# Placing matmuls and evictions one by one in an attention and experts kernel: turns in pairs, content next to the q terms, another layout for the position terms

## Chip, cores and metric

The kernel runs on one core of a Trainium2 chip. The metric is device time in microseconds (us) of the whole launch, the median of three runs. A profiled execution of the same kernel gives the trace; its own time is given beside its span, which runs from the first to the last instruction.

## What is computed

An adaptive layer norm, attention with relative position terms, a second norm and a mixture of experts, all in float32, with 16 sequences of 512 tokens, width 256, 16 heads of 16, and 8 experts of which each token uses two:

```python
h = layernorm(x) * (1 + ca) + sa
q, k, v = heads(h @ Wq + bq), heads(h @ Wk + bk), heads(h @ Wv + bv)
rel_q = einsum('bhld,lrd->bhlr', q, pos_emb)          # pos_emb[l, r] = dist_emb[l - r + 255]
rel_k = einsum('bhrd,lrd->bhlr', k, pos_emb)
scores = (q @ k.T + rel_q + rel_k) / sqrt(16)
x = x + ga * norm(softmax(scores) @ v @ Wo + bo + h)  # with gamma, beta
h = layernorm(x) * (1 + cb) + sb
x = x + gb * sum_over_the_two_best_experts(h @ w_e.T + b_e)
```

A negative index counts from the table's end, one beyond the end takes the last row.

## The kernel before

**Two stretches.** A first stretch norms the input, makes q, k and v and puts them into DRAM, turns q and k into stationary operands for the position terms (`stationary`), and computes the first ten blocks of these terms (`blocks`, LEAD = 10). Then comes the main loop, which works through 64 units. A unit is 128 query rows of one sequence. It goes through four groups g of four heads; t counts the heads of a group.

**Position terms.** `q_set` (L156) makes rel_q of 16 query rows in four banks of PSUM: 8 matmuls, two for each of four 32-row parts of TensorE (L165, bank names pq). ScalarE copies them to the tile r (L175). `k_set` (L177) makes rel_k with 16 matmuls into four banks pk (L186), and VectorE adds them to r (L195). `store` (L199) writes r to the DRAM tensor rel_d, one DMA of 1 MB for each quarter g. In the main loop each of the first 54 units also makes one block of these terms, ten units ahead of its use; the last ten make none.

**A group of heads.** `load_scores` (L577) reads the position terms of four heads into the tile s, one DMA of 1 MB. `content` (L637) makes q k^T of the four heads in four banks qk, each on 32 rows of TensorE (L644); VectorE adds s to each bank, scales, and takes the maximum (L650), then turns the maximum's sign (L654). `exps` (L657) is ScalarE's exponential in place. `turn` (L664) turns a head's 128 x 512 probabilities on TensorE, four 128 x 128 transposes into one bank pt (L669), and ScalarE copies them out as pT (L671). `context` (L674) multiplies by v, 16 matmuls of 32 columns into the bank pc (L684); a column of ones in v gives the sums of the softmax.

**A unit's rest.** `back` and `contextT` (pcl, pct) bring the context into the layout for the projection; `project` (ph, L727 and L732) adds h and multiplies by Wo, copies the sum out as x2 and starts the first norm; `residual`, `norm2` and `modulate` (fpt) give the experts' input, `route` (fpl) and `mask_t` (fpmt) the two chosen experts, `bias` (fpb) the biases, and `experts` the products with two experts at a time in the bank fpy (L827), four times a unit. `expert_sums` weighs one half on VectorE (L838) and one on ScalarE (L842). `sqrt_inv` (L99) raises to the power -1/2 on GpSimd (POOL), after an addition on VectorE (L100).

**Banks.** All but pc take their banks from one pool of seven; the eighth is pc's. Of the free banks a new tile gets the one that was released longest ago, in the order of the program.

**What sets the order.** The order is written by hand: every step has a slot and a rank in it, and the program is the list sorted by both. Each engine runs its own instructions in that order, and so does SP's queue, which issues nearly all DMAs. A unit starts a new round every 16 slots, so groups are four slots apart and steps of two or three units stand among one another (z is the unit's first slot, q0 a group's):

```python
            at(q0 - 12, 0, load_scores, u, g)
            at(q0 - 4, 5, content, u, g)
            at(q0 - 2, 7, exps, u, g, (0, 1))
            at(q0 - 1, 7, exps, u, g, (2, 3))
            for t in range(4):
                at(q0 + t, 3, turn, u, g, t)
            at(q0 + 5, 4, context, u, g)
```

with `q_set` at z + 2 + 4g (rank 4), `k_set` at z + 15 + 4g (rank 2), `experts` at z + 18 + 4 pr (rank 6) and `store` at z + 28 + 2g. In one slot, evictions stand directly behind the matmuls that they empty, since one function holds both.

Of the kernel before, what the change touches and what calls it, by code (L numbers as in the profile page):

```python
# [11 lines left out]
ALU = mybir.AluOpType  # L12
# [22 lines left out]
def adaln_attention_moe_kernel(  # L35
# [79 lines left out]
    rel_d = [dram.tile([P, P, S], F32, tag=f"rel_{n}", name=f"rel_d{n}") for n in range(8)]  # L115
# [10 lines left out]
    class Rel:  # L126
# [29 lines left out]
        def q_set(self, n, g):  # L156

            s, lb, rb, lh = self.at(n)
            e = self.qe[(lb * 2 + lh, g // 2)]
            bs = [bank(f"pq_{n}_{g}_{t}") for t in range(4)]  # L160
            for a in range(2):
                for t in range(4):
                    lp = lb * P + lh * LQ + 16 * g + 8 * a + 2 * t
                    m0 = S - 1 - lp + rb * RK
                    nc.tensor.matmul(  # L165
                        bs[t][:, a * 256 : (a + 1) * 256],
                        e[32 * t : 32 * t + 32, (g % 2) * 2 + a, :],
                        t_r[32 * t : 32 * t + 32, :, m0 : m0 + RK],
                        start=True, stop=True,
                    )  # L170
            dst = self.two[n % 2][:, 16 * g : 16 * g + 16, :].rearrange(
                "p (a t i) r -> p t a (i r)", a=2, t=4
            )
            for t in range(4):
                nc.scalar.copy(dst[:, t], bs[t].rearrange("p (a c) -> p a c", a=2))  # L175

        def k_set(self, n, g):  # L177
# [14 lines left out]
            for t in range(4):  # L192
                o = 32 * g + 8 * t
                dst = self.two[n % 2][:, :, o : o + 8]
                nc.vector.tensor_tensor(  # L195
                    dst, bs[t].rearrange("p (r l) -> p l r", r=8), dst, ALU.add
                )

        def store(self, n, g):  # L199

            s, lb, rb, lh = self.at(n)
            l0 = lh * LQ + 16 * g
            nc.sync.dma_start(
                out=rel_d[s * 4 + lb][:, l0 : l0 + 16, rb * RK : (rb + 1) * RK],
                in_=self.two[n % 2][:, 16 * g : 16 * g + 16, :],
            )
# [4 lines left out]
    with ExitStack() as pro:  # L211
# [163 lines left out]
        def blocks(n):  # L375
# [6 lines left out]
            for g in range(4):  # L382
                rel.q_set(n, g)
                for w in ahead:
# [3 lines left out]
            for g in range(4):  # L388
                rel.k_set(n, g)
                for w in ahead:  # L390
# [186 lines left out]
    def load_scores(u, g):  # L577
# [4 lines left out]
        nc.sync.dma_start(  # L582
            out=st, in_=rel_d[s * 4 + lb][h0 : h0 + 7 : 2].rearrange("h l r -> l h r")
        )
# [52 lines left out]
    def content(u, g):  # L637
# [4 lines left out]
        for t in range(4):  # L642
# [3 lines left out]
            )  # L646
        mx = u3.tile([P, 4], F32, tag="mx", name=f"mx_{u}_{g}")
# [16 lines left out]
    def turn(u, g, t):  # L664
        t_ = units[u]
        pt = bank(f"pt_{u}_{g}_{t}")
        for rb in range(NL):
            cols = slice(rb * P, (rb + 1) * P)
            nc.tensor.transpose(pt[:, cols], t_["s", g][:, t, cols], ident)  # L669
        pT = tp.tile([P, S], F32, tag="pT", name=f"pT_{u}_{g}_{t}")  # L670
        nc.scalar.copy(pT, pt)  # L671
# [49 lines left out]
    def project(u):  # L721
# [19 lines left out]
        nc.vector.bn_stats(stats, ph)  # L741
# [14 lines left out]
    def norm2(u):  # L756
# [6 lines left out]
        sqrt_inv(rstd, mv[:, 1:2], EPS_ADA)  # L763
        xn = u1.tile([P, E], F32, tag="xn", name=f"xn_{u}")
# [68 lines left out]
    def expert_sums(u, pr):  # L833
# [4 lines left out]
        nc.vector.scalar_tensor_tensor(  # L838
            t_["y"], py[:, 0:E], t_["mask"][:, e : e + 1], t_["y"], ALU.mult, ALU.add
        )  # L840
        ye = u2.tile([P, E], F32, tag=f"ye{pr > 0}", name=f"ye_{u}_{pr}")
        nc.scalar.activation(  # L842
            ye, py[:, E : 2 * E], AF.Identity, scale=t_["mask"][:, e + 1 : e + 2]
        )
# [13 lines left out]


    slots = {}  # L860

    def at(slot, order, fn, *args):
        slots.setdefault(slot, []).append((order, len(slots.get(slot, ())), fn, args))

    for u in range(NP):
        z = 16 * u
        for g in range(4):
            q0 = z + 4 * g
            at(q0 - 12, 0, load_scores, u, g)
            at(q0 - 4, 5, content, u, g)  # L870
            at(q0 - 2, 7, exps, u, g, (0, 1))
            at(q0 - 1, 7, exps, u, g, (2, 3))
            for t in range(4):
                at(q0 + t, 3, turn, u, g, t)
            at(q0 + 5, 4, context, u, g)
        at(z - 16, 0, lambda u: units.setdefault(u, {}), u)
        at(z - 13, 0, load_k, u, 0)
        at(z - 6, 0, load_k, u, 1)
        at(z - 15, 0, load_q, u)
        at(z - 7, 0, mask_q, u)  # L880
        at(z - 9, 0, load_rest, u)
        at(z + 15, 0, load_tail, u)
        z += 16
        at(z + 3, 6, back, u)
        at(z + 5, 3.5, contextT, u)
        at(z + 7, 6, project, u)
        at(z + 8, 0, residual, u)
        at(z + 10, 0, norm2, u)
        at(z + 11, 6, modulate, u)
        at(z + 13, 7, route, u)  # L890
        at(z + 15, 7, mask_t, u)
        at(z + 16, 7, bias, u)
        for pr in range(4):
            at(z + 18 + 4 * pr, 6, experts, u, pr)
            at(z + 19 + 4 * pr, 1, expert_sums, u, pr)
        at(z + 35, 0, finish, u)
# [3 lines left out]
        if n < NP:  # L900
            for g in range(4):
                at(z + 2 + 4 * g, 4, rel.q_set, n, g)
                at(z + 15 + 4 * g, 2, rel.k_set, n, g)
            for g in range(4):
                at(z + 28 + 2 * g, 0, rel.store, n, g)
        if n + 1 < NP:
            for w in rel.wants(n + 1):
                o = 8 + w[3] if w[0] == "q" else (16, 17, 21, 25)[w[2] % 2 * 2 + w[3]]
                at(z + o, 0, rel.load, w)
    for n in range(min(slots), max(slots) + 1):  # L910
        for _, _, fn, args in sorted(slots.get(n, ()), key=lambda e: e[:2]):
            fn(*args)
# [49 lines left out]
```

## Time and profile before

| | |
|---|---|
| Median of 3 runs | 2932.14 us (2932.07 to 2933.13) |
| Profiled execution: its time | 2935.72 us |
| Its span | 2934.0 us, mean granted TensorE clock 0.971 |
| Busy: TensorE (PE) | 2770.9 us, 94% |
| Busy: weight loads (PEld) | 1803.2 us, 61% |
| Busy: ScalarE (ACT) | 2068.8 us, 71% |
| Busy: VectorE (DVE) | 1837.4 us, 63% |
| Busy: GpSimd (POOL) | 630.1 us, 21% |
| DMA, SP's queue | 854,032 packets, 790.03 MB, 85.2% of 16 engines |
| rel_d<-r (stores) | 256 DMAs of 1,024 KB, 8.5 us to landing |
| s<-rel_d (loads) | 256 DMAs of 1,024 KB, 7.8 us to landing |

Groups that the change moves, from the page's table of costs: pT<-pt L671 1,024 times at 584 ns, r<-pk L195 1,024 at 683 ns, s<-s L660 1,024 at 731 ns, s<-qk L650 1,024 at 685 ns, r<-pq L175 1,024 at 603 ns.

How to read it: a row of a table of costs gives line, engine, operation, tiles (out<-in), shapes and count, then busy us and the mean of one. A row of the timeline gives start and length in us, engine, line and operation; several of a kind in a row are merged, and what stands in brackets is idle time of the engine before it and what ended it. The chain of waits is followed back from the last instruction; its pieces are cut where the next begins, so their lengths are times from start to start. Matmuls are pipelined, and TensorE's busy share contains short waits inside a group of matmuls.

### The profile page before, as it was taken

Reading aid. Unit: us, or ns where it says so; the run is one execution under the profiler, and the core shown is the slowest. Engines: PE = TensorE matmul, PEld = TensorE weight load, DVE = VectorE, ACT = ScalarE, POOL = GpSimd, SP = SyncE. Lnnn points to the kernel's source line nnn. Section 1 sums busy time; section 2 is a strip of 40 time slices with the busy share of each in tenths; the row PEclk is TensorE's granted clock in tenths of the full one; section 3 lists DMA queues with packets and bytes.
Section 4 is the critical chain, followed back from the end, with each engine's and each line's share of the span. In section 5 each row is a group of like instructions: output and inputs, shape, how many; then the busy total and the mean of one; then the engine's idle time right before and its main releaser. Section 6 shows DMA issues by size and latency. Waiting matters only on the chain.

```text
span 2934.0 us, 76492 instructions
## 1 busy us (share of the span) xinstructions
PE 2770.9 (94%) x30186; PEld 1803.2 (61%) x30186; DVE 1837.4 (63%) x5140; ACT 2068.8 (71%) x3938; POOL 630.1 (21%) x863
## 2 busy tenths in 40 slices
PE   8779963999999999999999999999999999999997
PEld 5556642666666666666666666666666666665654
DVE  5446542666666666666666666666666666675553
ACT  2345432877777777777777777777777777777774
POOL 1000000022222222222222222222222222223333
PEclk9989876999999999999999999999999999999998
DMA  6879998688988998899888998889899898897561
GB/s 181 306 253 317 296 299 273 223 276 283 286 282 277 294 307 279 274 285 292 281 278 286 291 289 281 278 285 288 278 286 307 279 286 281 278 278 264 201 238 43
DMA packets 855350, 796.49 MB, mean 271 GB/s; under 512 B 25545, under 2 KB 649409, under 8 KB 854737
## 3 DMA queue, kind: packets, MB, share of 16 engines
q1 hardware_dynamic: 854032, 790.03, 85.2%
q8 instruction: 240, 3.93, 0.5%
q10 hardware_dynamic: 960, 1.57, 0.2%
q14 instruction: 118, 0.96, 0.1%
HBM read 462.20 MB, written 328.25 MB: 269 GB/s over the span
## 4 chain that ended last, share of the span: by engine, by line
PE 77%; DMA 2%; POOL 2%; DVE 1%; SPq 1%; ACT 1%; issue 1%; POOLq 0%; DVEq 0%; ACTq 0%
PE pt L669 18%; PE fpy L827 15%; PE qk L644 12%; PE pq L165 10%; PE pc L684 8%; PE pk L186 8%; PE ph L732 2%; DMA vu<-v_d 1%; PE fpl L788 1%; PE pcl L699 1%; PE fpb L818 1%; PE fpt L775 1%; POOL qm L614 1%; PE pct L716 0%; POOL rstd L101 0%
## 5 line engine op out<-in xcount | busy, mean ns | idle before, releaser
L671 ACT COPY pT<-pt 128x512 f32<-128x512 f32 x1024 | 595.3, 584 | 317.9 <-PE pt L669 295.3
L195 DVE TENSOR_TENSOR r<-pk,r 128x512 f32<-128x512 f32 x1024 | 635.0, 683 | 189.2 <-PE pk L186 164.3
L660 ACT ACTIVATE s<-s,mx 128x512 f32<-128x512 f32 x1024 | 689.7, 731 | 43.3 <-DVE mx L654 39.7
L650 DVE CUSTOM_DVE_ANT_0 s<-qk,s 128x512 f32<-128x512 f32 x1024 | 644.1, 685 | 85.8 <-PE qk L644 81.4
L669 PE MATMUL pt<-ident,s 128*128 128x128 f32 x4096 | 660.0, 284 | 10.8 <-ACT s L660 10.4
L175 ACT COPY r<-pq 128x512 f32<-128x512 f32 x1024 | 525.6, 603 | 153.9 <-PE pq L165 137.1
L669 PEld LDWEIGHTS pt<-ident,s 128*128 128x128 f32 x4096 | 450.0, 143 | 284.7 <-ACT s L660 73.8
L827 PE MATMUL fpy<-we_sb,fhT 128*128 128x512 f32 x1024 | 506.1, 617 | 0.0
L848 POOL TENSOR_TENSOR ye<-ye,ye 128x256 f32<-128x256 f32 x192 | 140.5, 732 | 1597.4 <-ACT ye L842 1105.8
L838 DVE SCALAR_TENSOR_TENSOR fy<-fpy,fmask,fy 128x256 f32<-128x256 f32 x256 | 123.5, 482 | 471.6 <-PE fpy L827 319.3
L644 PE MATMUL qk<-k,qm 32*128 32x512 f32 x2048 | 380.1, 650 | 28.0 <-POOL qm L614 28.0
L186 PEld LDWEIGHTS pk<-t_f,ke 32*128 32x128 f32 x8192 | 268.3, 190 | 189.5 <-ACT r L175 124.1
L165 PE MATMUL pq<-t_r,qe 32*128 32x256 f32 x4096 | 370.5, 409 | 4.2 <-DMA qe<-eq_d 2.8
L186 PE MATMUL pk<-t_f,ke 32*128 32x128 f32 x8192 | 319.8, 287 | 8.8 <-DVE r L195 3.6
L827 PEld LDWEIGHTS fpy<-we_sb,fhT 128*128 128x128 f32 x1024 | 175.0, 190 | 195.2 <-issue 159.8
L165 PEld LDWEIGHTS pq<-t_r,qe 32*128 32x128 f32 x4096 | 240.2, 186 | 82.4 <-issue 41.7
L684 PE MATMUL pc<-pT,vu 128*32 128x128 f32 x8192 | 279.1, 277 | 0.0
L684 PEld LDWEIGHTS pc<-pT,vu 128*32 128x32 f32 x8192 | 209.9, 110 | 44.1 <-issue 43.5
L644 PEld LDWEIGHTS qk<-k,qm 32*128 32x128 f32 x2048 | 133.4, 184 | 101.5 <-DVE r L195 47.6
L101 POOL TENSOR_TENSOR rstd<-rstd,mhalf 128x1 f32<-128x1 f32 (+1 forms) x144 | 87.9, 610 | 436.0 <-DVE rstd L100 428.1
L842 ACT ACTIVATE ye<-fpy,fmask 128x256 f32<-128x256 f32 x256 | 125.3, 490 | 51.3 <-DVE fy L838 51.3
L614 POOL TENSOR_SCALAR qm<-qs,par 128x256 f32<-128x256 f32 x128 | 117.7, 932 | 150.1 <-DMA k<-k_d 137.8
(110 smaller groups left out, 2061.7 us busy)
## 6 DMA issues: line engine op xcount, KB each, us to landing
rel_d<-r SPq DMA_DIRECT2D x256, 1024.0 KB, 8.5
s<-rel_d SPq DMA_DIRECT2D x256, 1024.0 KB, 7.8
vu<-v_d SPq DMA_DIRECT2D x64, 576.0 KB, 7.5
ke<-ek_d SPq DMA_DIRECT2D x128, 256.0 KB, 7.2
k<-k_d SPq DMA_DIRECT2D x128, 256.0 KB, 6.6
gt<-gates_d SPq DMA_DIRECT2D x64, 256.0 KB, 4.7
v_d<-v SPq DMA_DIRECT2D x16, 576.0 KB, 6.4
xt<-in_x SPq DMA_DIRECT2D x16, 512.0 KB, 5.9
```

The source lines that it names most:

```text
L165: nc.tensor.matmul(bs[t][:, a * 256 : (a + 1) * 256], e[32 * t : 32 * t + 32, (g % 2) * 2 + a, :], t_r[32 * t : 32 * t + 32, :, m0 : m0 + RK],
L175: nc.scalar.copy(dst[:, t], bs[t].rearrange("p (a c) -> p a c", a=2))
L186: nc.tensor.matmul(bs[t][:, a * 128 : (a + 1) * 128], e[32 * t : 32 * t + 32, a, :], t_f[32 * t : 32 * t + 32, :, m0 : m0 + LQ], start=Tru ...
L195: nc.vector.tensor_tensor(dst, bs[t].rearrange("p (r l) -> p l r", r=8), dst, ALU.add)
L614: nc.gpsimd.tensor_scalar(qm[:, pa], qs, par[:, pa : pa + 1], None, ALU.mult)
L644: nc.tensor.matmul(bs[t], t_["q"][rows, pa, cc, :], t_["k", cc][rows, :], start=True, stop=True)
L650: nc.vector.tensor_tensor_reduce(st[:, t, :], bs[t], st[:, t, :], 0.25, -3.0e38, ALU.add, ALU.max, mx[:, t : t + 1],)
L660: nc.scalar.activation(t_["s", g][:, t, :], t_["s", g][:, t, :], AF.Exp, bias=t_["m", g][:, t : t + 1])
L669: nc.tensor.transpose(pt[:, cols], t_["s", g][:, t, cols], ident)
L671: nc.scalar.copy(pT, pt)
L684: nc.tensor.matmul(pc[32 * t : 32 * t + 32, g, :], t_["v"][:, rb, h * VW : h * VW + 32], pTs[t][:, rb * P : (rb + 1) * P], start=(rb == 0) ...
L827: nc.tensor.matmul(py, t_["hT"][:, kc, :], we_sb[:, kc, pr * 2 * E : (pr + 1) * 2 * E], start=(kc == 0), stop=(kc == NE - 1),)
```

## The change

Every step gets a position of its own on one number line, in slots as before, from a table O. The matmuls and the evictions of `q_set`, `k_set`, `content` and `turn` become steps of their own (`q_copy`, `k_add`, `add_content`, `turn_copy`), `exps` is placed head by head, and the second norm is cut in two (`norm2` ends at the power, `normed` applies it). In TensorE's order of a group, turns of heads 2 and 1 stand together, content stands directly ahead of the q terms, and turn 3 goes between experts and the k terms. The table also moves later steps of a unit, for example `modulate` from 11 to 13.3 and `finish`, which stores the output, from 35 to 42.1. In `expert_sums` ScalarE's half is put ahead of VectorE's in the program; as both read one bank, the second waits for the first. `project` takes the norm's statistics from x2 instead of the bank.

The DRAM tensor rel_d gets another layout, with blocks of 128 columns r outside the rows l. A quarter's store then writes 8 KB in one piece from each partition, where it wrote 16 pieces of 512 bytes. A load of four heads becomes four DMAs, each reading four pieces of 512 bytes for each partition, where one DMA read 2 KB pieces.

The first stretch uses the same functions in the same order as before, with the new layout.

```diff
-    rel_d = [dram.tile([P, P, S], F32, tag=f"rel_{n}", name=f"rel_d{n}") for n in range(8)]
+    rel_d = [dram.tile([P, NL, P, RK], F32, tag=f"rel_{n}", name=f"rel_d{n}") for n in range(8)]
...
                     )
+            self.qb = bs
+        def q_copy(self, n, g, ts):
             dst = self.two[n % 2][:, 16 * g : 16 * g + 16, :].rearrange(
...
             )
-            for t in range(4):
-                nc.scalar.copy(dst[:, t], bs[t].rearrange("p (a c) -> p a c", a=2))
+            for t in ts:
+                nc.scalar.copy(dst[:, t], self.qb[t].rearrange("p (a c) -> p a c", a=2))
...
                     )
-            for t in range(4):
+            self.kb = bs
+        def k_add(self, n, g, ts):
+            for t in ts:
                 o = 32 * g + 8 * t
...
                 nc.vector.tensor_tensor(
-                    dst, bs[t].rearrange("p (r l) -> p l r", r=8), dst, ALU.add
+                    dst, self.kb[t].rearrange("p (r l) -> p l r", r=8), dst, ALU.add
                 )
...
             nc.sync.dma_start(
-                out=rel_d[s * 4 + lb][:, l0 : l0 + 16, rb * RK : (rb + 1) * RK],
+                out=rel_d[s * 4 + lb][:, rb, l0 : l0 + 16, :],
                 in_=self.two[n % 2][:, 16 * g : 16 * g + 16, :],
...
                 rel.q_set(n, g)
+                rel.q_copy(n, g, range(4))
                 for w in ahead:
...
                 rel.k_set(n, g)
+                rel.k_add(n, g, range(4))
                 for w in ahead:
...
         st = sp.tile([P, 4, S], F32, tag="s", name=f"s_{u}_{g}")
-        nc.sync.dma_start(
-            out=st, in_=rel_d[s * 4 + lb][h0 : h0 + 7 : 2].rearrange("h l r -> l h r")
-        )
+        for t in range(4):
+            nc.sync.dma_start(
+                out=st[:, t, :].rearrange("p (rb r) -> p rb r", r=RK),
+                in_=rel_d[s * 4 + lb][h0 + 2 * t].rearrange("rb l r -> l rb r"),
+            )
         units[u]["s", g] = st
...
             )
+        t_["qk"] = bs
+    def add_content(u, g):
+        t_ = units[u]
+        bs = t_.pop("qk")
         mx = u3.tile([P, 4], F32, tag="mx", name=f"mx_{u}_{g}")
...
             nc.tensor.transpose(pt[:, cols], t_["s", g][:, t, cols], ident)
+        t_["pt", g, t] = pt
+    def turn_copy(u, g, t):
+        t_ = units[u]
         pT = tp.tile([P, S], F32, tag="pT", name=f"pT_{u}_{g}_{t}")
-        nc.scalar.copy(pT, pt)
+        nc.scalar.copy(pT, t_.pop(("pt", g, t)))
         t_["p", g, t] = pT
...
         mv = u2.tile([P, 2], F32, tag="mv", name=f"mv2_{u}")
-        nc.vector.bn_stats(stats, ph)
+        nc.vector.bn_stats(stats, x2)
         nc.vector.bn_aggr(mv, stats)
...
         sqrt_inv(rstd, mv[:, 1:2], EPS_ADA)
+        t_["ln2"] = (mv, rstd)
+    def normed(u):
+        t_ = units[u]
+        mv, rstd = t_.pop("ln2")
         xn = u1.tile([P, E], F32, tag="xn", name=f"xn_{u}")
...
         e = 2 * pr
-        nc.vector.scalar_tensor_tensor(
-            t_["y"], py[:, 0:E], t_["mask"][:, e : e + 1], t_["y"], ALU.mult, ALU.add
-        )
         ye = u2.tile([P, E], F32, tag=f"ye{pr > 0}", name=f"ye_{u}_{pr}")
...
             ye, py[:, E : 2 * E], AF.Identity, scale=t_["mask"][:, e + 1 : e + 2]
+        )
+        nc.vector.scalar_tensor_tensor(
+            t_["y"], py[:, 0:E], t_["mask"][:, e : e + 1], t_["y"], ALU.mult, ALU.add
         )
...
-    slots = {}
-    def at(slot, order, fn, *args):
-        slots.setdefault(slot, []).append((order, len(slots.get(slot, ())), fn, args))
+    O = {
+        "content": -2.4626,
+        "add_content": -2.3612,
+        ("exp", 0): -1.2159,
+        ("turn", 0): -0.8732,
+        ("exp", 2): -0.5643,
+        ("exp", 1): -0.4930,
+        ("turn_copy", 0): -0.4876,
+        ("turn", 2): 0.5281,
+        ("turn_copy", 2): 0.8703,
+        ("turn", 1): 1.4758,
+        ("turn_copy", 1): 1.4814,
+        ("exp", 3): 1.6823,
+        "q_set": 2.2208,
+        ("q_copy", 2): 2.4310,
+        ("q_copy", 3): 2.5904,
+        ("q_copy", 0): 2.7341,
+        ("q_copy", 1): 2.7393,
+        "back": 2.8935,
+        ("turn", 3): 2.9973,
+        ("turn_copy", 3): 3.3249,
+        "contextT": 3.9805,
+        "context": 4.1821,
+        "project": 5.8037,
+        "residual": 6.9000,
+        "norm2": 10.4317,
+        "normed": 10.8506,
+        "modulate": 13.3163,
+        "route": 14.5204,
+        "k_set": 15.0296,
+        ("k_add", 0): 15.0864,
+        ("k_add", 1): 15.5883,
+        ("k_add", 3): 15.5900,
+        ("k_add", 2): 15.6240,
+        "mask_t": 15.8852,
+        "bias": 18.0871,
+        "experts": 18.5363,
+        "expert_sums": 18.9734,
+        "store": 27.8101,
+        "finish": 42.0757,
+    }
+    pieces = []
+    def at(pos, fn, *args):
+        pieces.append((pos, len(pieces), fn, args))
...
         z = 16 * u
+        at(z - 16, lambda u: units.setdefault(u, {}), u)
+        at(z - 13, load_k, u, 0)
+        at(z - 6, load_k, u, 1)
+        at(z - 15, load_q, u)
+        at(z - 7, mask_q, u)
+        at(z - 9, load_rest, u)
+        at(z + 15, load_tail, u)
         for g in range(4):
             q0 = z + 4 * g
-            at(q0 - 12, 0, load_scores, u, g)
-            at(q0 - 4, 5, content, u, g)
-            at(q0 - 2, 7, exps, u, g, (0, 1))
-            at(q0 - 1, 7, exps, u, g, (2, 3))
+            at(q0 - 12, load_scores, u, g)
+            at(q0 + O["content"], content, u, g)
+            at(q0 + O["add_content"], add_content, u, g)
             for t in range(4):
-                at(q0 + t, 3, turn, u, g, t)
-            at(q0 + 5, 4, context, u, g)
-        at(z - 16, 0, lambda u: units.setdefault(u, {}), u)
-        at(z - 13, 0, load_k, u, 0)
-        at(z - 6, 0, load_k, u, 1)
-        at(z - 15, 0, load_q, u)
-        at(z - 7, 0, mask_q, u)
-        at(z - 9, 0, load_rest, u)
-        at(z + 15, 0, load_tail, u)
+                at(q0 + O["exp", t], exps, u, g, (t,))
+                at(q0 + O["turn", t], turn, u, g, t)
+                at(q0 + O["turn_copy", t], turn_copy, u, g, t)
+            at(q0 + O["context"], context, u, g)
         z += 16
-        at(z + 3, 6, back, u)
-        at(z + 5, 3.5, contextT, u)
-        at(z + 7, 6, project, u)
-        at(z + 8, 0, residual, u)
-        at(z + 10, 0, norm2, u)
-        at(z + 11, 6, modulate, u)
-        at(z + 13, 7, route, u)
-        at(z + 15, 7, mask_t, u)
-        at(z + 16, 7, bias, u)
+        for fn in (back, contextT, project, residual, norm2, normed, modulate, route, mask_t, bias):
+            at(z + O[fn.__name__], fn, u)
         for pr in range(4):
-            at(z + 18 + 4 * pr, 6, experts, u, pr)
-            at(z + 19 + 4 * pr, 1, expert_sums, u, pr)
-        at(z + 35, 0, finish, u)
+            at(z + O["experts"] + 4 * pr, experts, u, pr)
+            at(z + O["expert_sums"] + 4 * pr, expert_sums, u, pr)
+        at(z + O["finish"], finish, u)
...
             for g in range(4):
-                at(z + 2 + 4 * g, 4, rel.q_set, n, g)
-                at(z + 15 + 4 * g, 2, rel.k_set, n, g)
-            for g in range(4):
-                at(z + 28 + 2 * g, 0, rel.store, n, g)
+                q0 = z + 4 * g
+                at(q0 + O["q_set"], rel.q_set, n, g)
+                at(q0 + O["k_set"], rel.k_set, n, g)
+                for t in range(4):
+                    at(q0 + O["q_copy", t], rel.q_copy, n, g, (t,))
+                    at(q0 + O["k_add", t], rel.k_add, n, g, (t,))
+                at(z + O["store"] + 2 * g, rel.store, n, g)
         if n + 1 < NP:
...
                 o = 8 + w[3] if w[0] == "q" else (16, 17, 21, 25)[w[2] % 2 * 2 + w[3]]
-                at(z + o, 0, rel.load, w)
-    for n in range(min(slots), max(slots) + 1):
-        for _, _, fn, args in sorted(slots.get(n, ()), key=lambda e: e[:2]):
-            fn(*args)
+                at(z + o, rel.load, w)
+    for _, _, fn, args in sorted(pieces, key=lambda e: e[:2]):
+        fn(*args)
 # ---- launch: one core; the host lays the inputs out and no more ----
```

## The prediction, made before the run

> **What bounds the kernel now.** I read the chain of work that ended last, then TensorE in order of time, then the cost groups, then VectorE in order of time, then the windows.
>
> ```profile
> PE 77%; DMA 2%; POOL 2%; DVE 1%; SPq 1%; ACT 1%; issue 1%; POOLq 0%; DVEq 0%; ACTq 0%
> 1519.13 1.91 PE fpy L827 x4
> 1521.04 1.10 PE pk L186 x32
> 1522.15 0.59 PE pt L669 x4
> ...
> 1523.85 0.44 PE pt L669 x4
> 1524.28 1.07 PE qk L644 x8
> 1525.35 0.59 PE pt L669 x4
> 1525.94 1.01 PE pc L684 x32
> 1526.95 0.59 PE pt L669 x4
> 1527.54 1.95 PE pq L165 x15
> 1529.49 1.91 PE fpy L827 x4
> ```
>
> These are the chain and one group of four heads in it (left out: the unit's ph). TensorE is the chain, back to back; but pq took 1.95 here, and 1.08 at best. Over units in the steady stretch (700 to 2500 us, 39.13 us a unit, 52 alike) fpy, pk and pc never vary by over 0.01 us and pt by 0.06; pq averages 1.36 against 1.08, qk 1.51 (before a pt) against 1.07. Per unit that is 1.14 + 1.32 + 0.13 = 2.6 us of waiting, and 36.5 us of work.
>
> ```profile
> 1522.16 2.49 DVE L195 TENSOR_TENSOR r<-pk,r 128x512 f32<-128x512 f32 x4 [0.60 <-PE pk L186]
> 1526.39 0.68 DVE L650 CUSTOM_DVE_ANT_0 s<-qk,s 128x512 f32<-128x512 f32 x1
> 1527.00 0.69 DVE L650 CUSTOM_DVE_ANT_0 s<-qk,s 128x512 f32<-128x512 f32 x1
> 1527.61 0.69 DVE L650 CUSTOM_DVE_ANT_0 s<-qk,s 128x512 f32<-128x512 f32 x1
> ```
>
> What it waits for is banks: seven of them, and VectorE empties one per 0.61 us. In the instructions of that stretch the held-up pq began at 1528.36, 0.75 us after the add that started at 1527.61. So an eviction frees its bank 0.75 us after it starts, and TensorE is at fpy 1.06 us after the last of pq's four banks came.
>
> ```profile
> 340.00:480.00 140.00, 80.19 (x831) 63.99 (x824) 59.51 (x138) 41.49 (x80) 0.14 (x1) 0.70 0.95 283
> 700.00:2500.00 1800.00, 1799.95 (x21055) 1168.08 (x21048) 1215.04 (x3360) 1416.74 (x2717) 436.37 (x598) 1.00 0.91 285
> 465.68 9.65 SPq L203 DMA_DIRECT2D rel_d<-r  x4
> ```
>
> Two windows (length, PE, PEld, DVE, ACT, POOL busy, clock, DMA share) and one row of SP's queue. Before the main loop TensorE works 80 of 140 us with the DMA engines 95% busy, and SP needs 9.65 us to hand over four stores. In the main loop DMA is at 91%: second in line.
>
> **TensorE's order.** Per group, before: fpy, pk, pt, pt, qk, pt, pc, pt, pq. After, from the two instruction orders: pt2, pt1, qk, pq, fpy, pt3, pk, pt0, pc. Prices are start-to-start times. A pt between other tile shapes takes 0.59, entered only 0.49, left only 0.53, amid 128x128 work 0.44; so entering costs 0.05 and leaving 0.09 to 0.10. fpy is 1.91, and 1.72 between pts in the last units, where pk is gone: 0.1 each way.
> Before: 1.91 + 1.10 + 0.49 + 0.53 + 1.07 + 0.59 + 1.01 + 0.59 + 1.08 = 8.37. After, without waits: pt2 and pt1 1.02, qk and pq joined 1.07 + 1.08 − 0.21 = 1.94, fpy 1.82 (pt3 follows in its shape), pt3 0.53, pk 1.10, pt0 0.59, pc 1.01: 8.01. Saved: 0.36 a group, 1.44 a unit. But fpb and ph land between qk and pq, which breaks the join in two of four groups; with fpmt, pcl, pct, fpt and fpl in their new places I get 35.4 us of work a unit instead of 36.5.
>
> **The waits.** Banks go to whichever was released longest ago, so the builds tell whose bank each matmul inherits. qk now inherits pk banks and pt0's; pk ends 0.59 + 1.01 + 1.02 = 2.62 us before qk starts, and four k adds take 0.1 + 4 x 0.6. Only the fourth is near, and it goes to qk's last or to pq's first bank: the 1.32 us at qk go. What is late next is pq: its fourth bank is qk's own, first in groups 2 and 3, second in 0 and 1. VectorE's first add never starts earlier than 1.17 us after qk (idle VectorE, last units). So the bank comes at 1.17 + 0.75 = 1.92 us and fpy starts at 2.98 us after qk, not 1.94: a wait of 1.04. In group 0 the second add frees it: 2.53 + 1.06 = 3.59 against 0.96 + 0.52 + 1.08 = 2.56 with fpb: 1.03. In group 1, with ph, 3.59 against 3.30: 0.29. Sum 3.40.
> A unit after: 35.4 + 3.4 = 38.8 against 39.1, −0.3; over 52 units −16 us. Bounds: −1.0 a unit if the first add starts 0.2 us sooner, +0.5 if pq's first three banks come late too.
>
> A rule against this change stands in the Trainium skill, TensorEngine Tiling, Gotcha 1: row tiling raises PSUM pressure, since row tiles write different banks. By the drain rule of the same page (Key Properties) alone, which says a change of tiling mode drains TensorE, the sum would be 35.4 + 2.6 = 38.0, −59 us. The rows say qk and pq together want eight banks of seven, so I take 38.8.
>
> **Evictions and norms.** Their number stays: 1,024 each of exps, pT copies, q copies, k adds, content adds, at 0.73, 0.58, 0.60, 0.68, 0.69. ACT's order per group is now q copies 2, 3, 0, 1, exp0 of the next group, ye, pT3, exp2, exp1, pT0, pT2, pT1, exp3. From qk's start: copies 2.7 to 4.7, exp0 to 5.4 (its maximum is there at 3.9), ye 5.9, pT3 6.4, exp2 7.1, exp1 7.7, pT0 8.3; TensorE asks for exp2 at 8.0, exp1 at 8.5, pT0's bank at 9.0. All hidden, least slack 0.7 us. ACT is 79% busy. The swapped expert sum makes VectorE wait for ye: 5.9 + 0.5 = 6.4, and pk ends at 6.4. Behind it stand four k adds; they have 1.2 us until the next content add, so 0. bn_stats reading x2 instead of PSUM: 0.42 and 0.41 in the two rows, 0; it now waits for the copy, which ends before the adds ahead of it do. The second norm in two steps: in the order nothing of VectorE's stands between them in that group, so its 1.18 us wait for POOL stays, under TensorE: 0. The later out store (slot 42 for 35) takes away SP's wait for POOL; nobody waits for it: 0.
>
> **DMA.** In the trace's packets, 512 B took 27 ns (mean 28.7), 2 KB 84 (96), 8 KB 309 (337). A store was 2,048 packets of 512 B: 3.67 us of the 16 engines; it becomes 128 of 8 KB: 2.5 to 2.7. A load was 512 of 2 KB: 3.09; it becomes four DMAs, 2,048 of 512 B: 3.67. Four of each per unit: −4.2 + 2.3 = −1.9 us of about 36, so DMA stays second. Twelve more issues a unit at 0.40 us on SP are 4.8 us; SP now idles over 10 us a unit at its first store, and what is queued behind (loads, later stores) has over 9 slots of 2.4 us before use: 0. The skill (DMA: Bandwidth & Descriptors, Measured and its fit for GpSimd's queue) speaks against it: batch to 1 MiB, about 2 us fixed per DMA. If those added up, 12 x 2 = 24 us a unit on 36 would be 60, +1,080 us. But SP issues 256 KB loads 0.45 us apart while several are in flight, so I take the row.
> In the stretch before the loop the same saving counts. Sixteen stores are issued from 357 to 472 us; 16 x 1.05 = 17, less 2 for the first loads: −15. Between −4 (only the last four) and −40 (all forty).
>
> **Last units.** Without q and k terms ten units take 29.4 us each. There exp0 follows qk by 3.9 us, and pt0 now comes right after fpy and pt3 (3.4), so the loop is ACT's: 3.9 + exp0 0.7, ye 0.5, pT3 0.55, exp2 0.67, exp1 0.67, pt1 0.6 = 7.6 a group, 30.4 a unit. The 2 us wait for xn at fpt (pt L669 before it took 2.47) is gone within that. +1 x 10 = +10; bounds −10 and +25.
>
> Sum: −16 − 15 + 10 = −21 us. The profiled execution took 2935.7 us, 3.6 above the median of three; 2914.7 there is about 2911 in the median. I say **2912**.
>
> **Rivals.** (a) The bank wait is covered, because the first adds run before all four row tiles end: then 38.0 or less a unit, −59 − 15 + 10 = −64: 2868. For: those adds stand at the head of VectorE's queue when qk ends. Against: the four qk start within 0.02 us and end together; no add started before 1.16. 0.09. (b) Slower: VectorE's expert sum, queued before the k adds, waits for ACT's ye. From 1.3 us later than I have it, k adds push the next content adds, and each further 0.1 us costs 208 x 0.1 = 21 us; with the gains elsewhere it decides at about 1.4 us. At 1.5 us late: 0.2 x 208 = +42 on the sum: 2954. For: ACT has twelve steps in order with little slack. Against: 0.7 us or more at each. 0.27. (c) DMA binds on 512 B reads at SP's issue: 40 us a unit, +0.9 x 52 − 15 + 10: 2974. For: 91% now. Against: stores get cheaper by more. 0.04. (d) It does as the sum says but the last units or the first stretch take it back: within 0.2%, 0.17. The sum as written: 0.43.
>
> **Numbers.** A measurement of this kernel can tell about 0.2% (5.9 us) from no change. Faster: 0.43 + 0.09 = 0.52; same 0.17; slower 0.27 + 0.04 = 0.31. The likeliest case alone: 2890 to 2926. The range for 8 in 10 reaches to (a) below and through most of (b) above: 2864 to 2964.
>
> **What would show it.** qk's waits gone, pq standing about 2 us from qk's start to its last bank (start-to-start of qk and pq together 3.0); fpy 1.82 before pt3; units of 38.8; DMA share about 0.87; the first unit's start some 15 us earlier; last units at 30 to 31 us with pt0 waiting for exp0. Wrong if units are under 38.3 or over 39.3, or if VectorE's wait for ye shows among the longest.

## The result and the profile after

The changed kernel takes 2913.43 us (median of four runs, 2910.37 to 2915.89) beside 2932.11 us before (four runs on the same chip). The ratio is 0.9937, with a 95% interval of 0.992 to 0.9954. Its profiled execution took 2910.4 us, with a span of 2908.6 us and a mean clock of 0.976.

The starts of the transposes pcl of the 1st, 53rd and 64th unit cut each trace into four parts. Each number is a difference of start times in the two traces (not all of the 52 units have the steady length):

| part (us) | before | after | difference | forecast |
|---|---|---|---|---|
| start to the first unit | 538.0 | 521.4 | −16.6 | −15 |
| the next 52 units (one steady unit) | 2030.8 (39.11) | 2016.1 (38.83) | −14.7 | −16 |
| the last eleven intervals | 329.4 | 339.6 | +10.2 | +10 |
| after the last pcl | 35.8 | 31.6 | −4.2 | none |
| span | 2934.0 | 2908.6 | −25.4 | −21 |

First the shares of the chain of waits of the changed kernel by engine, and one group of four heads in it, in order of time (start, length, what):

```profile
PE 75%; DVE 3%; issue 2%; DMA 2%; ACT 1%; SPq 1%; POOL 0%; DVEq 0%; POOLq 0%; ACTq 0%
1542.62 1.11 PE qk L654 x8
1543.73 0.02 DVE s L665
...
1544.46 1.13 PE pq L165 x10
1545.59 1.91 PE fpy L851 x4
1547.50 0.44 PE pt L684 x4
1547.94 1.10 PE pk L189 x32
```

Before, the chain ran through TensorE back to back. Now it steps from qk to VectorE's content add, which starts 1.11 us after qk, and comes back to TensorE at pq, 0.75 us after the add's start (1543.71 in the next view). The rest is back to back with the lengths of the forecast (by the starts of the records fpy takes 1.82 and the turn behind it 0.53; the chain cuts this pair at 1.91 and 0.44).

VectorE in the same stretch, in order of time:

```profile
1543.71 0.69 DVE L665 CUSTOM_DVE_ANT_0 s<-qk,s 128x512 f32<-128x512 f32 x1 [1.21 <-PE qk L654]
...
1548.31 0.48 DVE L866 SCALAR_TENSOR_TENSOR fy<-fpy,fmask,fy 128x256 f32<-128x256 f32 x1
1549.06 1.29 DVE L201 TENSOR_TENSOR r<-pk,r 128x512 f32<-128x512 f32 x2 [0.26 <-PE pk L189]
```

VectorE was idle for 1.21 us when qk's products came, so it is not VectorE's load that delays the bank. The expert sum L866 is ahead of the k adds, and these wait for pk, not for it.

Then the rows of the weight loads of qk and pq among the costliest groups (busy and mean ns, then idle time ahead and what ended most of it), first of the kernel before, then of the changed one:

```profile
L644 PEld LDWEIGHTS qk<-k,qm 32*128 32x128 f32 x2048 | 133.4, 184 | 101.5 <-DVE r L195 47.6
L165 PEld LDWEIGHTS pq<-t_r,qe 32*128 32x128 f32 x4096 | 240.2, 186 | 82.4 <-issue 41.7
```

```profile
L654 PEld LDWEIGHTS qk<-k,qm 32*128 32x128 f32 x2048 | 81.1, 184 | 66.8 <-issue 32.6
L165 PEld LDWEIGHTS pq<-t_r,qe 32*128 32x128 f32 x4096 | 317.7, 186 | 179.7 <-DVE mx L665 91.9
```

Before, qk waited for the k adds (L195). Now the longest wait is at pq, ended by the content adds. The two windows that were shown of before (columns as there):

```profile
340.00:480.00 140.00, 79.69 (x812) 63.05 (x811) 60.60 (x145) 42.31 (x82) 1.98 (x3) 0.67 0.86 304
700.00:2500.00 1800.00, 1784.36 (x21171) 1207.95 (x21167) 1228.98 (x3389) 1409.11 (x2737) 439.54 (x602) 1.00 0.92 287
```

And the four stores on SP's queue:

```profile
453.61 3.06 SPq L209 DMA_DIRECT2D rel_d<-r  x4
```

Ahead of the loop the DMA engines fell from 0.95 to 0.86 busy, and SP hands over four stores in 3.06 us where it needed 9.65. In the loop DMA is at 0.92, not at the 0.87 of the forecast.

The last units need one more look. The same group of four heads in two of these units of the kernel before, in the columns of the windows above:

```profile
2685.14:2693.18 8.04, 8.04 (x66) 5.03 (x65) 4.39 (x17) 5.52 (x12) 0.73 (x1) 0.79 0.44 157
2715.22:2721.69 6.47, 6.47 (x66) 4.15 (x65) 4.29 (x17) 5.52 (x12) 0.72 (x1) 1.00 0.53 190
```

The work is the same, but the clock that TensorE was granted was 0.79 in the first and 1.00 in the second. Four groups of the last units ran at 0.79, and each took some 1.57 us longer, 6.3 together. At full clock a unit there took 28.5 us, and with one such group 30.1. In the trace of the changed kernel no group of the last units is below 1.00. So the new order costs 1.9 us a unit there (30.4 against 28.5), and the clock gives back 6.3 us over the stretch. Why the clock falls in these groups is open. The kernel with the new layout alone also has four such units.

### The profile page after: what moved, and what is told of

The parts are those of the page before. It is cut to its first block, busy times and chain, and to the rows that moved or that the text cites. A ratio compares the mean times of both kernels' runs of the same rounds, so it can differ in the third digit from the quotient of the medians.

```text
span 2908.6 us, 78285 instructions
## 1 busy us (share of the span) xinstructions
PE 2740.0 (94%) x30186; PEld 1839.1 (63%) x30186; DVE 1844.9 (63%) x5140; ACT 2042.8 (70%) x3938; POOL 629.8 (22%) x863
## 3 DMA queue, kind: packets, MB, share of 16 engines
q10 hardware_dynamic: 960, 1.57, 0.2%
## 4 chain that ended last, share of the span: by engine, by line
PE 75%; DVE 3%; issue 2%; DMA 2%; ACT 1%; SPq 1%; POOL 0%; DVEq 0%; POOLq 0%; ACTq 0%
PE pt L684 17%; PE fpy L851 14%; PE pq L165 12%; PE qk L654 9%; PE pc L703 9%; PE pk L189 8%; DVE s L665 2%; PE ph L751 2%; PE fpl L812 1%; ACT s L675 1%; PE pcl L718 1%; DMA s<-rel_d 1%; PE ph L746 1%; PE fpb L842 1%; SPq L591 1%
## 5 line engine op out<-in xcount | busy, mean ns | idle before, releaser
L675 ACT ACTIVATE s<-s,mx 128x512 f32<-128x512 f32 x1024 | 727.4, 741 | 101.6 <-DVE mx L669 101.6
L690 ACT COPY pT<-pt 128x512 f32<-128x512 f32 x1024 | 586.2, 592 | 145.6 <-PE pt L684 142.2
L684 PE MATMUL pt<-ident,s 128*128 128x128 f32 x4096 | 614.4, 281 | 32.3 <-ACT s L675 30.9
L684 PEld LDWEIGHTS pt<-ident,s 128*128 128x128 f32 x4096 | 456.6, 141 | 220.5 <-issue 94.0
L165 PE MATMUL pq<-t_r,qe 32*128 32x256 f32 x4096 | 482.2, 409 | 23.9 <-DVE mx L665 19.6
L165 PEld LDWEIGHTS pq<-t_r,qe 32*128 32x128 f32 x4096 | 317.7, 186 | 179.7 <-DVE mx L665 91.9
L654 PE MATMUL qk<-k,qm 32*128 32x512 f32 x2048 | 294.6, 643 | 23.0 <-DMA s<-rel_d 23.0
L866 DVE SCALAR_TENSOR_TENSOR fy<-fpy,fmask,fy 128x256 f32<-128x256 f32 x256 | 123.0, 481 | 105.2 <-ACT ye L863 103.1
L654 PEld LDWEIGHTS qk<-k,qm 32*128 32x128 f32 x2048 | 81.1, 184 | 66.8 <-issue 32.6
```

The lines of the kernel that those rows point to most:

```text
L165: nc.tensor.matmul(bs[t][:, a * 256 : (a + 1) * 256], e[32 * t : 32 * t + 32, (g % 2) * 2 + a, :], t_r[32 * t : 32 * t + 32, :, m0 : m0 + RK],
L654: nc.tensor.matmul(bs[t], t_["q"][rows, pa, cc, :], t_["k", cc][rows, :], start=True, stop=True)
L675: nc.scalar.activation(t_["s", g][:, t, :], t_["s", g][:, t, :], AF.Exp, bias=t_["m", g][:, t : t + 1])
L690: nc.scalar.copy(pT, t_.pop(("pt", g, t)))
```

## The experiments

### Each half alone: layout, and order

The first kernel is the one before with only these lines of the change; the second is the changed one with these lines taken back.

```diff
-    rel_d = [dram.tile([P, P, S], F32, tag=f"rel_{n}", name=f"rel_d{n}") for n in range(8)]
+    rel_d = [dram.tile([P, NL, P, RK], F32, tag=f"rel_{n}", name=f"rel_d{n}") for n in range(8)]
-                out=rel_d[s * 4 + lb][:, l0 : l0 + 16, rb * RK : (rb + 1) * RK],
+                out=rel_d[s * 4 + lb][:, rb, l0 : l0 + 16, :],
-        nc.sync.dma_start(
-            out=st, in_=rel_d[s * 4 + lb][h0 : h0 + 7 : 2].rearrange("h l r -> l h r")
-        )
+        for t in range(4):
+            nc.sync.dma_start(
+                out=st[:, t, :].rearrange("p (rb r) -> p rb r", r=RK),
+                in_=rel_d[s * 4 + lb][h0 + 2 * t].rearrange("rb l r -> l rb r"),
+            )
```

> The kernel before, with only the new layout of rel_d (stores in 8 KB pieces, loads as four DMAs of 512 B pieces). Theory (the layout pays only ahead of the main loop, because TensorE binds in the loop): units stay at 39.1 us, last units at 29.4, first unit starts some 15 us earlier; 2932 - 15 = 2917, ratio 0.995. Rival (the whole gain is TensorE's order, the layout does nothing): first unit where it was, 2932. Second rival (the layout also frees something in the loop): units under 39.0.

> The changed kernel with the old layout of rel_d. Theory: units 38.8, last units 30.4, first unit starts where it did before (538 us); -16 in the loop, +10 in the last units: 2926, ratio 0.998. Rival (all of the gain is the order): 2913. Second rival (DMA, which is then at 0.95 or more of the loop, binds): units 39 or longer, 2935.

Layout alone: 2919.14 us (five runs), ratio 0.996 (0.9946 to 0.9973). Its units stayed at 39.11, its last intervals at 328.9 together; the first unit started at 522.0. Order alone: 2926.03 us (eleven runs), ratio 0.9986 (0.9977 to 0.9996), units 38.83, last intervals 342.3, first unit at 534.0. Of the 2929.71 us that the kernel before took there, 0.4% are 11.7 us and 0.14% are 4.1 us, together 15.8; the change as a whole gave 0.63%, 18.5 us (13.5 to 23.5). So both parts are clear of zero, the order's only just, and they add up within the interval. The start of the first unit varies between traces: in three with the old layout it was at 531.5 to 538.0, in eleven with the new one at 519.4 to 525.4. The means differ by 12.5 us, a better figure for the layout than the 16.6 of one pair. The clock is not the reason: two kernels of the last experiment, which differ in the layout alone, have a mean clock of 0.87 up to there both, and start the first unit at 520.1 and 531.5.

With the order alone the last intervals took 342.3 us and not 339.6. One group makes nearly all of it (10.38 us for 7.77): its content add waits 3.82 us for a load of position terms, and its clock is 0.85.

### The bank wait, with a bank less

> The changed kernel, which leaves out the q terms of one 32-row part in four (head part t = 3: no product, no copy; its places in r hold zeros from the start), so that pq takes three banks instead of four. Theory (the wait in the changed order is for pq's fourth bank, which is qk's own): the wait of VectorE at L665 by pq goes, fpy starts 1.9 to 2.1 us after qk instead of 2.97, units 35.4 to 36.2, and DMA is then near 1.0 of the loop, so it may set 35.7 to 36.5 itself; about 2913 - 52 x 2.9 = 2762. Rival (the wait is not the bank's; TensorE just takes that long for pq behind qk): units shorten by 0.0 to 0.5 us only, 2890 to 2913.

```diff
-            bs = [bank(f"pq_{n}_{g}_{t}") for t in range(4)]
+            bs = [bank(f"pq_{n}_{g}_{t}") for t in range(3)]
-                for t in range(4):
+                for t in range(3):
```

It took 2782.01 us (two runs), with units of 36.42. A part of its chain, in order of time (its L656 is content, its L167 pq):

```profile
1518.31 1.07 PE qk L656 x8
1519.38 0.86 PE pq L167 x12
1520.24 1.91 PE fpy L853 x4
```

Content goes straight over into pq, and fpy comes 1.93 us after qk where it took 2.96. The time that pq itself needs did not shrink with its work: behind ph it took 1.07 us with 12 matmuls, and 1.08 is the least with 16 in the trace of before. So what left is waiting: by start times 1.03 us in group 2, 0.58 in group 3, 0.62 in group 0 and 0.18 in group 1, together 2.4, the whole difference of the units. In group 0 fpb takes the free bank, and pq still waits for one of qk's; that is why the units missed the expected 35.4 to 36.2 by 0.2. The rival, under which TensorE needs that long behind qk anyway, is out.

### Small edits that were costed at nothing

> The changed kernel with three of its small edits undone: VectorE's half of the expert sum stands first again, the norm's statistics are read from the bank, and the output is stored at slot 35 again. Theory (these three are hidden under TensorE and cost nothing): units 38.8, 2913 within 6. Rival (the swapped halves make VectorE late, which costs 0.1 us a group and more): 2890 or less.

It took 2983.88 us (four runs, ratio 1.0187, 1.017 to 1.0204): undone together, the three cost 70 us, and without them the change would be a loss. The theory and its rival both missed. Two kernels part the edits.

```diff
+        nc.vector.scalar_tensor_tensor(
+            t_["y"], py[:, 0:E], t_["mask"][:, e : e + 1], t_["y"], ALU.mult, ALU.add
+        )
         ye = u2.tile([P, E], F32, tag=f"ye{pr > 0}", name=f"ye_{u}_{pr}")
         nc.scalar.activation(
             ye, py[:, E : 2 * E], AF.Identity, scale=t_["mask"][:, e + 1 : e + 2]
         )
-        nc.vector.scalar_tensor_tensor(
-            t_["y"], py[:, 0:E], t_["mask"][:, e : e + 1], t_["y"], ALU.mult, ALU.add
-        )
```

> The changed kernel with only VectorE's half of the expert sum ahead of ScalarE's again (one of the three edits of e5_small_undo, which took 71 us more). Theory, formed on the trace of e5 (ScalarE's half then waits for VectorE's, which stands behind VectorE's wait for GpSimd's power in the norms; behind ScalarE's half stand a turn's copy and two exponentials that the last units wait for): units 39.0, last units 35 to 38, 2975 to 2985. Rival (it is the output's store at slot 35, or the statistics read from the bank): 2913.

```diff
-        nc.vector.bn_stats(stats, x2)
+        nc.vector.bn_stats(stats, ph)
-        "finish": 42.0757,
+        "finish": 35.0,
```

> The changed kernel with only the other two edits of e5_small_undo undone: statistics from the bank, the output stored at slot 35. Theory (they cost nothing): 2913 within 6, units 38.8, last units 30.4. Rival: 2975 to 2985.

The order of the halves is all of it: 2984.65 us (1.0179, 1.0161 to 1.0197), while statistics and store gave 2911.39 (0.9936). The spans of the two traces differ by 74.9 us: 59.4 lie in the last eleven intervals, 6.9 in the 52 units, and 4.0 and 4.5 ahead of the first unit and behind the last pcl, where traces vary. Of the 59.4, some 12 us come from eight groups whose granted clock was 0.78 to 0.91; the rest is at full clock. ScalarE, VectorE and TensorE of the kernel with the halves alone (its L866 is ScalarE's half, its L862 VectorE's) in one group of the last units, in order of time:

```profile
2712.46 0.72 ACT L675 ACTIVATE s<-s,mx 128x512 f32<-128x512 f32 x1 [2.51 <-DVE mx L669]
2714.69 0.47 ACT L866 ACTIVATE ye<-fpy,fmask 128x256 f32<-128x256 f32 x1 [1.51 <-DVE fy L862]
2715.06 0.58 ACT L690 COPY pT<-pt 128x512 f32<-128x512 f32 x1
```

```profile
2713.85 0.41 DVE L789 TENSOR_SCALAR xn<-x,mv,rstd 128x256 f32<-128x256 f32 x1 [0.69 <-POOL rstd L101]
2714.18 0.48 DVE L862 SCALAR_TENSOR_TENSOR fy<-fpy,fmask,fy 128x256 f32<-128x256 f32 x1
```

```profile
2715.69 1.61 PE L703 MATMUL pc<-pT,vu 128*32 128x128 f32 x26 [1.45 <-ACT pT L690]
```

ScalarE in the same kind of group of the changed kernel:

```profile
2713.32 0.72 ACT L675 ACTIVATE s<-s,mx 128x512 f32<-128x512 f32 x1 [2.51 <-DVE mx L669]
2713.95 0.46 ACT L863 ACTIVATE ye<-fpy,fmask 128x256 f32<-128x256 f32 x1
2714.31 0.58 ACT L690 COPY pT<-pt 128x512 f32<-128x512 f32 x1
```

Read from TensorE back: context waits 1.45 us for turn 3's copy; the copy stands behind ye; ye waits 1.51 us for VectorE's half in the same bank; that half stands behind the norm, which waits for GpSimd (this group, of 11.01 us, is one of those with a lower clock; at full clock it takes 9.39). In the four groups of a unit ye waits 1.48, 1.51, 1.01 and 0.40 us for VectorE: behind the two norms, behind the choice of the experts, and behind the context's scaling. At full clock these groups are 1.6, 1.6, 1.1 and 0.6 us longer than in the changed kernel. So GpSimd has a part in two of them only; what counts is all that VectorE does between the maximum and its half of the sum. With ScalarE's half first the first link is cut: ye follows the exponential at once, and the copy comes 1.0 us after the exponential's start instead of 2.6. VectorE's half then waits for ye (103 us over the kernel), and nothing that TensorE needs stands near enough behind it.

### How late ye may be

The same rival from the other side: ye is moved back in ScalarE's order, VectorE's half and all k adds with it.

```diff
-        "expert_sums": 18.9734,
+        "expert_sums": 19.3800,
-        ("k_add", 0): 15.0864,
+        ("k_add", 0): 15.3900,
```

(19.5100 and 15.5110 in the second kernel.)

> The changed kernel with ScalarE's half of the expert sum (ye) one step later in ScalarE's order, behind the copy of turn 3 (about 1.0 us later), with VectorE's half and all four k adds behind it as before. In the trace of the changed kernel VectorE has 1.2 to 1.4 us between its last k add and the next content add. Theory (the cost is nothing up to 1.3 us of lateness): units 38.8, 2913. Rival (every delay of ye reaches TensorE): +0.8 us a group, 40 us or more on a unit count of 52: 3080.

> The same with ye two steps later still, behind the exponentials of heads 2 and 1 (ye then ends some 2.4 us later than in the changed kernel). From the loop of its trace: content add at 0, exp0 3.45, turn copy 4.1 to 4.6, two exponentials to 6.1, ye 6.6, VectorE's half 7.1, four k adds to 9.6, against a group of 9.26: 0.3 to 0.5 us a group too long. Theory (slope 1 behind the threshold): units 40.0 to 40.8, last units 1 to 2 us shorter each, as ye leaves their loop: 2960 to 3005. Rival (VectorE's queue has more slack than that, or the exponentials move forward to make up for it): 2895 to 2915.

The first took 2906.69 us (two runs), units 38.83 and last intervals 3.8 us shorter together; the second 2997.24 (two runs), units 40.49. Its last units are 29.9, 0.5 shorter and not 1 to 2. Over the steady groups, counted from each group's qk:

| | ye ends at (median) | last k add to next content add |
|---|---|---|
| changed kernel | 6.34 | 1.21 to 1.43 |
| ye behind turn 3's copy | 7.05 | 0.68 to 1.07 |
| ye behind two exponentials more | 8.48 | −0.09 to 0.08 |

VectorE in the last of these, in order of time:

```profile
1506.15 0.48 DVE L866 SCALAR_TENSOR_TENSOR fy<-fpy,fmask,fy 128x256 f32<-128x256 f32 x1 [3.17 <-ACT ye L863]
1506.56 2.48 DVE L201 TENSOR_TENSOR r<-pk,r 128x512 f32<-128x512 f32 x4
1508.95 0.68 DVE L665 CUSTOM_DVE_ANT_0 s<-qk,s 128x512 f32<-128x512 f32 x1
```

There is no gap left: the expert sum waits 3.17 us for ye, the k adds follow it, and the content add follows them. That is rival (b) of the prediction, with its threshold where the slack ends. The changed kernel is some 1.2 us away from it.

### A run of four turns

If pq waits for content's banks, other work belongs between the two. This order has context between content and pq, and the four turns in one run (positions of turns, their copies, exponentials 1 to 3, `context`, `project` and `residual` changed, VectorE's half first, statistics from the bank):

```diff
-        ("turn", 0): -0.8732,
+        ("turn", 0): -0.7000,
-        ("turn", 2): 0.5281,
+        ("turn", 2): -0.6000,
-        ("turn", 1): 1.4758,
+        ("turn", 1): -0.5000,
-        ("turn", 3): 2.9973,
+        ("turn", 3): 3.2000,
-        "context": 4.1821,
+        "context": 5.6000,
```

> The changed kernel with another order: all four turns in one run (pt3, pt0, pt2, pt1), and context between content and the q terms, where it covers the wait for content's banks; VectorE's half of the expert sum first again, statistics from the bank. Theory: pc (1.0 us) stands where TensorE waited 1.04 us, so most of 3.4 us of waits a unit goes; the join of qk and pq is given up (+0.2 a group), the run of four turns saves 0.1: about 36.2 us a unit, 52 x 2.6 = 135 us, 2780, with DMA at 0.98. Rival 1 (DMA binds before): units 36.5 to 37.5. Rival 2 (a run of four turns asks for exps and banks faster than ScalarE gives them, each turn then waits 0.1 to 0.4 us): units 38 to 40, 2870 to 2980.

> The order of e4_one_run with the old layout of rel_d. Theory (the layout pays only ahead of the loop, even at a unit of 37.6): units 37.6 to 37.8, first unit some 12 us later: 2855. Rival (at 0.95 of the loop the DMA engines begin to bind, and the old layout costs there): units 38 or more, 2870 to 2890.

> The order of e4_one_run, with ScalarE's half of the expert sum first and the other small edits as in the changed kernel. Theory: in its loop TensorE waits for pq's bank 0.24 us a group, whatever ScalarE does, so units stay 37.5 to 37.6; in the last units ScalarE's half waited 0.3 to 0.4 us a group for VectorE's, which goes: 29.2 to 28.0 each, 12 us, 2832. Rival (the expert sum's order matters in the loop too): units 37.0 or less, 2815.

> The order of e4_one_run with ScalarE's half of the expert sum first, and directly behind exp0 as in the changed kernel, not behind three exponentials as in e11; statistics as in e4. Theory (what e11 lost came from the place of ScalarE's half, not from the swap as such): the waits of VectorE's half for ye that e11 showed go, units 37.4 to 37.8 as in e4, where pq's bank sets them; last units 28.4 as in e11: 2830 to 2840. Rival (in this order any wait of VectorE for ScalarE delays the k adds): units 39 or more, 2910.

The first took 2843.34 us (four runs), ratio 0.9708 (0.9694 to 0.9723): the best of all kernels here. Its units are 37.65, not 36.2. A group of it, on TensorE in order of time:

```profile
1521.49 1.26 PE qk L654 x8
1522.74 1.01 PE pc L703 x32
1523.76 1.31 PE pq L165 x15
```

Three terms are longer than the expectation had them. fpy comes 1.31 to 1.33 us after pq's start where 1.08 would do: in this order pq inherits two of qk's banks in every group, and the second add frees its bank only some 2.5 us after qk. qk to pc takes 1.24 to 1.26, in one group 1.37, where I had 1.07. And the four turns take 0.1 to 0.3 us more than their prices in three of four groups. Its DMA share in the loop is 0.95. With the old layout it took 2857.5 (0.9763, 0.9747 to 0.9779), units still 37.65 and the first one 11 us later: at this pace too the layout pays nothing in the loop. The last intervals are 2.2 us longer, nearly all in one unit right behind the loop. There a load waits for the last store, and a content add for the load, in order of time along the chain:

```profile
2565.38 8.40 DMA rel_d<-r
2573.86 5.56 DMA s<-rel_d
2579.55 0.69 DVE s L663
```

The third and fourth kernel missed. With ScalarE's half first (and the other small edits of the change) this order took 3024.16 us (1.0318, 1.0299 to 1.0336), units 41.13. TensorE's turns in it, by the row of the costliest groups (the idle time stands behind the second bar; in the first kernel of this section it was 17.4):

```profile
L684 PE MATMUL pt<-ident,s 128*128 128x128 f32 x4096 | 593.5, 283 | 108.2 <-DVE fy L866 96.3
```

Here turn 2 takes the bank of the experts' product, so the expert sum stands on TensorE's path; ye comes behind three exponentials, and VectorE's half behind ye. VectorE also waited 168 us (700 to 2500 us) for the copy x2, from which the statistics are read. With ye directly behind exp0 and the statistics from the bank again, the fourth kernel took 2857.06 (0.9743, 0.9727 to 0.9759), with units of 37.92, and VectorE waiting 529 us for ye in all. These two edits were made together, so what each gave back is open. With both, this kernel is still 10 to 14 us slower than the first (0.9743 against 0.9708), 17 us above its theory; its rival, with units of 39 and 2910 us, was further off. It differs from the first in the place of ye too, so this is no pure test of the swap. In this order the swap gained nothing at either of the two places that were tried, where it saves 71 us in the changed kernel's.

## Why the prediction was right, point by point

- **TensorE's work and waits.** Right. The forecast had fpy 2.98 us after qk in groups 2 and 3 and 3.59 in groups 0 and 1; the trace has 2.96 to 2.97, 3.59 and 3.58. fpy to turn 3 is 1.82, turn 3 0.53, pk 1.10, turn 0 0.59. The unit is 38.83 where 38.8 was said (before it is 39.11; the forecast read 39.13). The cause (pq's fourth bank is qk's own, and comes 0.75 us after an add that never starts sooner than 1.16 us after qk) is what the kernel with three banks shows. The sum by the drain rule alone, 38.0, kept the old 2.6 us of waits and came out 0.8 too low. In the Trainium skill, TensorEngine Tiling, Gotcha 1 (row tiling increases the pressure on PSUM) was the rule to follow: here the pressure cost 2.4 us a unit by the kernel with three banks.
- **DMA in the loop.** Wrong in size. The step said a store of 2.5 to 2.7 us and a load of 3.67, and a share of 0.87. By the packets of the trace, 8 KB took 309 ns at the median but 360 in the mean (a tenth took 522 or more), and 512 B 29.65: a store is 128 x 360 / 16 = 2.88, a load 2,048 x 29.65 / 16 = 3.80. Four of each save 4 x (6.76 − 6.68) = 0.3 us a unit, not 1.9. It cost no time, as TensorE sets the loop. The fixed part of about 2 us for each DMA (the Trainium skill, DMA: Bandwidth & Descriptors, Anatomy of one DMA, there for GpSimd's queue) did not add up on SP's queue, as the prediction held: twelve more loads a unit left the unit at 39.11 with the layout alone, and a load landed in 6.2 us instead of 7.8.
- **First stretch.** Right: −15 against −16.6 in the pair of traces and −12.5 between the means.
- **Last units.** The number was right, the base and the loop were not. The forecast took 29.4 us as the length of a unit; that is a mean over units of 28.5 at full clock and some of 30.1 or more. It then added 1.0 a unit, where at full clock it is 1.9. That the sum still came to +10 is luck: the granted clock, of which the forecast had no term, gave back 6.3 us. As for the loop, the forecast made it ScalarE's: exp0, ye, turn 3's copy, exp2, exp1, pt1, 7.6 a group. Had it been so, taking ye out from there would have given 2 us a unit; the kernel with ye behind exp1 has 29.9 instead of 30.4. The chain of the changed kernel shows another loop:

```profile
2709.46 1.11 PE qk L654 x8
...
2713.12 0.18 DVE mx L669
2713.32 0.73 ACT s L675
...
2714.10 0.66 PE pt L684 x4
2714.75 1.25 PE pc L703 x32
2716.00 0.59 PE pt L684 x4
2716.58 0.22 PE fpt L799 x2
2716.80 0.44 PE pt L684 x4
2717.24 1.11 PE qk L654 x8
```

  qk to the maximum 3.8, exp0 0.8, then turn 0, context and two turns on TensorE, 0.65 + 1.25 + 1.03: 7.56 without fpt. ye counts only as far as it delays turn 3's copy, for which context waits (1.25 instead of 1.01).
- **Edits costed at nothing.** Statistics and store: right. VectorE's wait for GpSimd in the second norm is 0.69 us, not the 1.18 that was to stay, and costs nothing either way. The swapped expert sum: the step looked at what the swap makes wait, VectorE for ye, and priced that rightly at 0. That wait is among VectorE's longer ones (103 us, the fourth of its waits), which the forecast named as a sign of being wrong; it was none, since 1.2 us of slack stand behind it. The step did not ask what the swap frees, ScalarE from VectorE: undone, that costs 71 us. The total came out because the forecast's list for ScalarE had ye straight behind exp0, which holds only with the swap. The sign of the whole change hangs on it.
- **The end.** Not in the forecast: after the last pcl 4.2 us were gained. What gave it is open: with VectorE's half first it is 36.1 us there, as before, but with all three edits undone 34.7, and with the new order and the old layout 33.9; and the mean clock there differs between the traces (0.78 before, 0.86 after, 0.75 with the halves alone undone).
- **Rivals.** (a) did not happen: over all 256 groups the first add starts 1.16 us after qk or later. (b) is real and lies some 1.2 us away, where the prediction had 1.3 to 1.4. (c) did not bind, though DMA stood at 0.92 and not at 0.87.

Open: what the second norm in two steps does alone was not tried, and no run shows why the clock falls in some groups of the last units.

## What to carry to other kernels

When two matmuls in parts of 32 rows are put next to each other, count the banks that both hold: when they are more than are free, the second waits for the first one's eviction, and work that needs no new bank belongs between them. Before costing an edit at nothing, ask for each engine what stands directly behind the moved instruction, in the old order and in the new one: in these kernels two readers of one bank kept the program's order, and the engine that came second inherited all that the first one waited for. A faster transfer pays where something waits for it: here ahead of the loop, and once behind it, but not in the loop. Before taking a mean over units as the length of one, look at the units one by one, with the clock of each.

## What the runs showed of the hardware

- The first content add starts 1.16 us after the first record of qk at the least, over 256 groups in each of three kernels (before, changed, four turns in one run), with VectorE idle for 1.21 us ahead of it in the row above. That the four products in parts of 32 rows end together would explain it; no run shows it directly.
- 8 KB packets have a long tail: median 309 ns, mean 360, while 512 B packets had 27 and 29.65. Larger pieces of the stores, with smaller ones of the loads, moved the loop's DMA share from 0.91 to 0.92.
- Content to context takes 1.24 to 1.37 us, while content to a turn takes 1.07; the reason is open.
- With the same 66 matmuls a group took 6.47 us at a granted clock of 1.00 and 8.04 at 0.79.
